# Division moved behind the values' product for the last two tiles of layers 2 and 3, and layer 3's first norm moved ahead in layer 2's quantised product

## The chip, the cores and the metric

One Trainium2 chip, and of it one core. The program is one launch; its metric is the device time of that launch in microseconds (us). The core has five engines with an instruction queue each: PE (TensorE, matrix products; the profile shows its weight loads apart, as PEld), DVE (VectorE), ACT (ScalarE), POOL (GpSimd) and SP (SyncE, which starts transfers). Work that has to cross from one engine to another waits on a semaphore.

## What is computed

Eight steps on x, 4 sequences of 256 tokens with 256 features: four layers, each a gated attention over 64 context tokens and a gated feed-forward part. The change lies in layers 2 and 3:

```python
x = x + tanh(g_xattn[2]) * _L2_xattn_ref(_layernorm(x), ctx, ...)
x = x + tanh(g_ffn[2])   * _L2_ffn_ref(_layernorm(x), weight, bias)
x = x + tanh(g_xattn[3]) * _L3_xattn_ref(_layernorm(x), ctx, ...)     # as layer 2
x = x + tanh(g_ffn[3])   * _L3_ffn_ref(_layernorm(x), ...)            # 8 experts, 2 chosen, 1 shared

def _L2_xattn_ref(q, latent_kv, Wq, Wkv_expand, Wout):                # 16 heads of 16
    qp = q @ Wq.T;  k, v = jnp.split(latent_kv @ Wkv_expand.T, 2, axis=-1)
    scores = jnp.einsum('bhqd,bhkd->bhqk', qh, kh) * inv_sqrt_d
    scores = jnp.where(causal, scores, jnp.finfo(scores.dtype).min)
    out = jnp.einsum('bhqk,bhkd->bhqd', jax.nn.softmax(scores, axis=-1), vh)
    return out.transpose(0, 2, 1, 3).reshape(b, sq, H) @ Wout.T

def _L2_ffn_ref(x, weight, bias):       # int8 rows of x times int8 rows of weight
    x_scale = jnp.maximum(jnp.max(jnp.abs(x), axis=2, keepdims=True) / 127, 1e-12)
    x_q = jnp.clip(jnp.round(x / x_scale), -128, 127)
    return (x_q @ w_q.T) * x_scale * w_scale + bias
```

## The kernel before

**Tiles.** The 1024 tokens are 8 tiles `x[0]` to `x[7]` of 128 tokens by 256 features, which stay in on-chip memory. Tiles 0 to 3 are group 0, tiles 4 to 7 group 1. A norm (`layernorm`, L427) works on a group: statistics on DVE (L432, L435), the root, then the scaling on DVE (L455) or, with `scalar=True`, on ACT (L448 the shift on DVE, L452 on ACT). The root is taken on ACT (L441), or with `powered=True` as a power on POOL (L438, L439).

**Attention in layers 2 and 3** (`attention23`). For each tile: `scores` (L1115 on PE; L1130 maximum and L1132 subtraction on DVE; L1141 exponential on ACT), `weights` (L496 sum over the 64 keys and L497 reciprocal, both on DVE; L501 the multiplication by it, 128x1024 values, on POOL), `transposed_pairs` (8 transposes, L516 on PE, and two copies out of PSUM, L517 on ACT), `context` (the product with the values, L1148 on PE in 8 products of 32 columns each, which the profile shows as 16 instructions; copied out by ACT at L1157) and `output` (L1165 on PE), which `gated_add` (L527 on DVE) adds to x. In the last tile the multiplication L501 is shared: heads 0 to 7 on DVE, 8 to 15 on POOL.

**Order.** `in_flight_parts` (L543) writes the order out by hand: in its turn i it starts the scores of tile i, the weights of tile i-1, and the transposes and context of tile i-2. Up to tile 4 the output follows its own context at once; from tile 6 on it comes after the transposes of the tile behind it. Beside it run generators: in layer 2 the keys and values of layer 3, and in the last turns the norm and the rounding of group 0 for the quantised product (`beside2`). The framework's planner then makes one fixed queue for each engine: what comes first in the program goes first, except where the planner's own timing finds it not ready and something later ready. `behind(a, b)` forces a to stand after b. `kept_busy(n, ...)` puts n products on PE whose result nobody reads.

**The quantised product between them** (`ffn2`, L2062). Group 0 was already rounded in attention 2. Its whole numbers are transposed (L2071 on PE, L2072 on ACT), multiplied (L2080 on PE, `unit`), scaled (L2084 on DVE) and added to x (L2085 on POOL). Then 7 filling products. Then group 1: `rounded(1)` takes its norm, its largest values (L2048), the reciprocal (L2050), the rounding (L2053, L2055, DVE) and adds the bias to x (L2059, POOL); its transposes; then the norm of layer 3 for group 0, then `unit(1, ...)` with 2 filling products, and last the transposes of that norm (L467 on PE, L169 and L171 out) and the queries of layer 3 for group 0 (L482 on PE, L1074 on ACT). Layer 3's first scores need those queries.

**Buffers.** Normed tiles, `y` and `ctxTok` share 7 buffers (tag `xn`), `attn` and `attnT` share 6 (tag `t4`), products in PSUM use 4 single buffers (`mm`) and 2 double ones (`wide`).

## Time and profile before

| what | value |
|---|---|
| median of 3 executions | 822.75 us (818.82, 822.75, 823.13) |
| the profiled execution | 820.13 us, of which the span is 818.3 us |
| PE busy | 773.3 us, 94% of the span |
| DVE, ACT, POOL busy | 502.3, 291.1, 242.9 us |
| granted TensorE clock, mean | 0.996 of full |
| layer 2's scores begin on PE | near 538 us |
| layer 2's last addition to x (L527) | 583.62 us |
| layer 3's first scores (L1115) | 602.70 us |
| layer 3's last addition to x | 646.11 us |
| PE busy, 660 to 680 us | 20.00 of 20 us |

Times inside the span are counted from its start. A row of a timeline gives the start, the length, the engine, the line, the operation, what it writes and reads, how many instructions are merged into the row, and in brackets how long the engine had stood idle and what ended that. A row of waits gives who waited for whom, the sum, the number of waits and the longest. A row of groups gives the busy time and the mean of one instruction in ns.

### The profile page before, as it was taken

The numbers are of one execution on the slowest core, as the hardware profiler recorded it, in microseconds if no ns is written. First come the engines' busy times: TensorE is split into PE (matmuls) and PEld (weight loads), VectorE is DVE, ScalarE is ACT, GpSimd is POOL, SyncE is SP. The second block draws the span as 40 slices with busy tenths as digits, with TensorE's granted clock in tenths as the row PEclk, the third lists the DMA queues.
The fourth block names the chain that finished last, engine by engine and source line by source line (L and its number), as shares of the span: only waits on it lengthen the run. The fifth ranks groups of instructions, "written<-read, shape, count | busy, mean of one in ns | idle before, by whom it ended". The sixth has DMA issues, their size and how long they took to land. (4 is left out here: it accounts for less than half of the span.)

```text
span 818.3 us, 12520 instructions
## 1 busy us (share of the span) xinstructions
PE 773.3 (94%) x4509; PEld 519.4 (63%) x4512; DVE 502.3 (61%) x1154; ACT 291.1 (36%) x506; POOL 242.9 (30%) x214
## 2 busy tenths in 40 slices
PE   6999999899999899999999989999898899999994
PEld 5544433787565677676656565855445647999993
DVE  5565455876694455543878859889879664344331
ACT  2221111443421333332543459166555421233320
POOL 1454544231113244322022110015524103444332
PEclk9999999999999999999999999999999999999998
DMA  9510114800021253333740000450000102222211
GB/s 341 202 40 0 40 58 162 280 37 25 27 65 49 62 123 69 76 79 78 278 177 1 8 1 27 162 204 1 27 0 2 52 9 85 53 48 40 29 18 16
DMA packets 32467, 62.44 MB, mean 76 GB/s; under 512 B 5552, under 2 KB 19504, under 8 KB 31696
## 3 DMA queue, kind: packets, MB, share of 16 engines
q1 hardware_dynamic: 25008, 51.91, 18.5%
q0 software_dynamic: 7104, 9.41, 6.9%
q8 instruction: 39, 0.64, 0.3%
q10 hardware_dynamic: 288, 0.26, 0.1%
q14 instruction: 28, 0.23, 0.1%
HBM read 52.81 MB, written 9.27 MB: 76 GB/s over the span
## 5 line engine op out<-in xcount | busy, mean ns | idle before, releaser
L501 POOL TENSOR_TENSOR attn<-attn,sm 128x1024 f32<-128x1024 f32 (+1 forms) x32 | 55.9, 1750 | 220.4 <-DVE sm L497 176.2
L482 PE MATMUL wide<-xT,big 128*128 128x512 f32 (+1 forms) x240 | 108.6, 600 | 1.1 <-DVE shared L1724 0.9
L782 DVE TENSOR_TENSOR rope<-wide,big 128x512 f32<-128x512 f32 x96 | 59.6, 684 | 52.0 <-PE wide L482 52.0
L482 PEld LDWEIGHTS wide<-xT,big 128*128 128x128 f32 (+1 forms) x240 | 43.4, 188 | 57.3 <-issue 49.3
L1497 PE MATMUL wide<-blk,still 128*128 128x128 f32 x640 | 74.8, 275 | 0.6 <-DVE blk L1469 0.6
L1497 PEld LDWEIGHTS wide<-blk,still 128*128 128x128 f32 x640 | 73.1, 192 | 0.8 <-issue 0.8
L754 PE MATMUL mm<-vo,attnT 128*128 128x256 f32 x256 | 58.6, 382 | 1.6 <-ACT attnT L517 1.2
L482 PE MATMUL wide<-xT,dense 128*128 128x512 f32 (+1 forms) x120 | 55.2, 599 | 0.1
L754 PEld LDWEIGHTS mm<-vo,attnT 128*128 128x128 f32 x256 | 47.8, 190 | 11.5 <-issue 3.0
L517 ACT COPY attnT<-mm 128x512 f32<-128x512 f32 x64 | 34.5, 587 | 37.5 <-PE mm L516 37.1
L496 DVE TENSOR_REDUCE sm<-attn 128x16 f32<-128x1024 f32 x32 | 38.6, 1208 | 12.9 <-ACT attn L490 11.6
L1459 DVE COPY still<-big 128x1024 f32 x20 | 13.9, 693 | 52.0 <-PE wide L1497 44.5
L1531 POOL DMA_INDIRECT out_dram<-ring,scratch x20 | 31.5, 1577 | 39.5 <-DVE ring L1524 15.8
L1531 POOL DMA_INDIRECT sums<-ring,big x17 | 26.8, 1578 | 48.3 <-ACT ring L1613 18.9
L516 PE MATMUL mm<-ident,attn 128*128 128x128 f32 x256 | 34.5, 276 | 5.7 <-POOL attn L501 2.8
L1515 PE MATMUL mm<-big,hidden 128*128 x160 | 37.8, 380 | 1.4 <-DVE hidden L1508 1.4
L1432 POOL DMA_INDIRECT xs<-xd,scratch x20 | 20.0, 1000 | 62.2 <-PE mm L1466 34.1
L516 PEld LDWEIGHTS mm<-ident,attn 128*128 128x128 f32 x256 | 28.7, 141 | 14.6 <-issue 6.1
L1507 ACT ACTIVATE hidden<-wide 128x512 f32<-128x512 f32 x20 | 12.0, 598 | 71.2 <-PE wide L1497 65.7
L482 PEld LDWEIGHTS wide<-xT,dense 128*128 128x128 f32 (+1 forms) x120 | 21.5, 185 | 24.7 <-issue 22.3
L527 DVE SCALAR_TENSOR_TENSOR x<-mm,tg,x 128x256 f32<-128x256 f32 x44 | 20.6, 473 | 21.4 <-PE mm L754 12.7
L836 ACT COPY big<-mm 128x512 f32<-128x512 f32 x16 | 8.6, 589 | 68.0 <-PE mm L824 61.7
(367 smaller groups left out, 1581.8 us busy)
## 6 DMA issues: line engine op xcount, KB each, us to landing
big<-in_L_w_gate_up SPq DMA_DIRECT2D x8, 1024.0 KB, 10.4
big<-in_L_w_down SPq DMA_DIRECT2D x8, 512.0 KB, 10.7
w_L_qk<-in_L_qk SPq DMA_DIRECT2D x4, 896.0 KB, 9.6
big<-in_L_w SPq DMA_DIRECT2D x2, 1480.0 KB, 8.1
big<-in_L_w SPq DMA_DIRECT2D x2, 1110.0 KB, 5.4
big<-in_L_wo SPq DMA_DIRECT2D x1, 2048.0 KB, 15.0
big<-in_L_w SPq DMA_DIRECT2D x2, 1024.0 KB, 5.1
xd<-xn SPq DMA_DIRECT2D x16, 128.0 KB, 1.8
```

Of the source, the lines that this page charges most:

```text
L482: nc.tensor.matmul(ps, w(c), xT[:, c, :], start=(c == 0), stop=(c == 1))
L496: nc.vector.tensor_reduce(sm, e, AX.X, ALU.add)
L501: engine.tensor_tensor(one, one, sm[:, part].unsqueeze(2).to_broadcast(list(one.shape)), ALU.mult)
L516: nc.tensor.transpose(ps[:, i * P : (i + 1) * P], ev[:, pr * P : (pr + 1) * P], ident)
L517: nc.scalar.copy(aT[:, half * 4 : half * 4 + 4, :].rearrange("p i t -> p (i t)"), ps)
L527: return nc.vector.scalar_tensor_tensor(x[t], ps, gate, x[t], ALU.mult, ALU.add)
L754: nc.tensor.matmul(ps[:, :D], aT[:, s, :], vo[:, s, :], start=(s == 0), stop=(s == NP - 1))
L782: nc.vector.tensor_tensor(m[:, s, :].rearrange("q (b t) -> q b t", t=S), ps[:, s, :].rearrange("q (b t) -> q b t", t=S), table, ALU.mult,)
L1432: nc.gpsimd.indirect_dma_start(out=xs, out_offset=None, in_=self.xd, in_offset=bass.IndirectOffsetOnAxis(ap=self.gather[:, b : b + 1].bitc ...
L1497: made = nc.tensor.matmul(ps[:, k, f : f + P], w[:, at : at + P], st[:, c * P : (c + 1) * P], start=(c == 0), stop=(c == 1),)
L1515: made = nc.tensor.matmul(ps[:, :D], hT[:, j * P : (j + 1) * P], self.w[:, bass.ds(r + j * D, D)], start=(j == 0), stop=(j == n - 1),)
L1531: nc.gpsimd.indirect_dma_start(out=self.sums[b % len(self.sums)], out_offset=bass.IndirectOffsetOnAxis(ap=self.scatter[:, b : b + 1].bitca ...
```

## The change

It has three parts.

1. For tiles 6 and 7 of layers 2 and 3, `weights` is not called: the exponentials are transposed undivided. In `context`, behind the product with the values, 8 more products with a constant matrix of zeros and ones (`pair_ones`, 32 columns) put each head's sum, 16 times over, into the other half of the same PSUM buffer; DVE takes the reciprocal of that 128x256 block and multiplies. These take the place of ACT's copy (L1157).
2. The order in `in_flight_parts`: both last tiles are transposed one after the other, and from tile 3 on the output of a tile comes behind the transposes of the next and ahead of its context. In layer 2 one filling product is put ahead of tile 6's context.
3. In `ffn2`, the rounding is split from the scales, and layer 3's norm for group 0 stands ahead of group 1's rounding, and its transposes ahead of `unit(1, ...)`. The 2 filling products behind that unit are left out. The shift of group 1's norm is put behind group 0's second `y`.

```diff
+    pair_ones = const.tile([P, 32], F32, tag="pair_ones", name="pair_ones")
+    nc.gpsimd.memset(pair_ones, 0.0)
+    nc.gpsimd.memset(pair_ones[:64, :16], 1.0)
+    nc.gpsimd.memset(pair_ones[64:, 16:], 1.0)
...
-            nc.vector.scalar_tensor_tensor(shift, mv[:, :, 0], -1.0, rstd, ALU.mult, ALU.mult)
+            made = nc.vector.scalar_tensor_tensor(shift, mv[:, :, 0], -1.0, rstd, ALU.mult, ALU.mult)
+            if late is not None:
+                behind(made, late)
...
-            if 1 <= i <= NT:
-                sums = weights(made[i - 1], shared=i == NT)
+            if 1 <= i <= NT - 2:
+                weights(made[i - 1])
             t = i - 2
-            if 0 <= t < NT:
+            if 0 <= t < NT - 1:
                 aT = turn(made.pop(t))
-            if t >= NT - 2:
+            if t == NT - 2:
+                last = turn(made.pop(NT - 1))
+            if t == NT - 1:
+                aT = last
+            if t >= TPG:
                 add(t - 1)
-                made_x = gated_add(t - 1, outs.pop(t - 1)[:, :D], gate)
-                if t == NT - 2:
-                    behind(made_x, sums)
+                gated_add(t - 1, outs.pop(t - 1)[:, :D], gate)
             if 0 <= t < NT:
                 ctx[t] = context(t, aT)
-            if 0 <= t < NT - 3:
+            if 0 <= t < TPG - 1:
                 add(t)
...
         def context(t, aT):
+            if layer == 2 and t == NT - 2:
+                kept_busy(1, ps_wide()[:, 0], kept["out"])
...
+            if t >= NT - 2:
+                for pr in range(NP):
+                    half, r = divmod(pr, 4)
+                    nc.tensor.matmul(
+                        ps[r * 32 : (r + 1) * 32, 2 * P + half * P : 2 * P + (half + 1) * P],
+                        pair_ones, aT[:, pr, :], start=True, stop=True, tile_position=(0, r * 32),
+                    )
+                nc.vector.reciprocal(cT, ps[:, 2 * P :])
+                nc.vector.tensor_tensor(cT, ps[:, : 2 * P], cT, ALU.mult)
+                return cT
...
-            kept_busy((7, 2)[g], ps_wide()[:, 0], last)
+            if g == 0:
+                kept_busy(7, ps_wide()[:, 0], last)
...
-        xq, xs = rounded(1)
-        xqT = turned(xq)
-        xn = layernorm(0, True)
+        xn, xi, xs = rounded(1, after_y=True)
+        xn_3 = layernorm(0, True)
+        xqT = turned(integers(xn, xi))
+        xT_3 = transposed(xn_3)
         unit(1, xqT, xs)
-        kept[3, 0] = head_queries(3, transposed(xn))
+        kept[3, 0] = head_queries(3, xT_3)
```

`integers` is the loop of L2053 and L2055, taken out of `rounded`; the additions of the bias (L2059) now stand ahead of it in the program.

More of the change, by code (lines that the diff above doesn't have):

```diff
@@ L424, in keep_rows, with layernorm @@
             nc.sync.dma_start(out=tiled(sums, layer)[:, t, :], in_=x[t])
-    def layernorm(g, scalar=False, after=(), powered=False):
+    def layernorm(g, scalar=False, after=(), powered=False, late=None):
         mv = small([P, TPG, 2], "mv")
@@ L516, in transposed_pairs @@
                 nc.tensor.transpose(ps[:, i * P : (i + 1) * P], ev[:, pr * P : (pr + 1) * P], ident)
-            nc.scalar.copy(aT[:, half * 4 : half * 4 + 4, :].rearrange("p i t -> p (i t)"), ps)
+            kept["turned"] = nc.scalar.copy(aT[:, half * 4 : half * 4 + 4, :].rearrange("p i t -> p (i t)"), ps)
         return aT
@@ L1156, in context @@
             cT = sb.tile([P, 2 * P], F32, tag="xn", name="ctxTok", bufs=AHEAD + 2)
+            if t >= NT - 2:
[3 more added lines that the diff above has]
+                        ps[r * 32 : (r + 1) * 32, 2 * P + half * P : 2 * P + (half + 1) * P],
+                        pair_ones,
+                        aT[:, pr, :],
+                        start=True,
+                        stop=True,
+                        tile_position=(0, r * 32),
+                    )
+                nc.vector.reciprocal(cT, ps[:, 2 * P :])
+                nc.vector.tensor_tensor(cT, ps[:, : 2 * P], cT, ALU.mult)
+                return cT
             made = nc.scalar.copy(cT, ps[:, : 2 * P])
@@ L1164, in output @@
             for half in range(2):
-                nc.tensor.matmul(
+                kept["out"] = nc.tensor.matmul(
                     ps[:, :D], cT[:, half * P : (half + 1) * P], w_o[:, half, :], start=(half == 0), stop=(half == 1)
@@ L1178, in beside2 @@
             if i == NT + 1:
-                kept["rounded"] = rounded(0, xn)
+                xn, xi, xs = rounded(0, xn)
+                kept["rounded"] = integers(xn, xi), xs
             next(keys, None)
@@ L2039, in weights2, with rounded @@
         return wqT, scale, bias
-    def rounded(g, xn=None):
+    def rounded(g, xn=None, after_y=False):
         bias = kept["weights2"][2]
-        xn = xn or layernorm(g, True, powered=True)
+        xn = xn or layernorm(g, True, powered=True, late=kept["y"] if after_y else None)
         xs = small([P, TPG], "xs")
@@ L2050, in rounded, with integers @@
         nc.vector.reciprocal(xi, xs)
+        for i in range(TPG):
+            t = g * TPG + i
+            nc.gpsimd.tensor_tensor(x[t], x[t], bias, ALU.add)
+        return xn, xi, xs
+    def integers(xn, xi):
         whole_numbers = []
@@ L2056, in rounded @@
             whole_numbers.append(q)
-        for i in range(TPG):
-            t = g * TPG + i
-            nc.gpsimd.tensor_tensor(x[t], x[t], bias, ALU.add)
-        return whole_numbers, xs
+        return whole_numbers
     def ffn2(gate):
@@ L2083, in unit @@
                 y = sb.tile([P, D], F32, tag="xn", name="y", bufs=AHEAD + 2)
-                nc.vector.scalar_tensor_tensor(y, ps[:, :D], xs[:, i : i + 1], scale, ALU.mult, ALU.mult)
+                made = nc.vector.scalar_tensor_tensor(y, ps[:, :D], xs[:, i : i + 1], scale, ALU.mult, ALU.mult)
+                if i == 1:
+                    kept["y"] = made
                 nc.gpsimd.tensor_tensor(x[t], x[t], y, ALU.add)
-            kept_busy((7, 2)[g], ps_wide()[:, 0], last)
+            if g == 0:
+                kept_busy(7, ps_wide()[:, 0], last)
         xq, xs = kept.pop("rounded")
         unit(0, turned(xq), xs)
-        xq, xs = rounded(1)
-        xqT = turned(xq)
-        xn = layernorm(0, True)
+        xn, xi, xs = rounded(1, after_y=True)
+        xn_3 = layernorm(0, True)
+        xqT = turned(integers(xn, xi))
+        xT_3 = transposed(xn_3)
         unit(1, xqT, xs)
-        kept[3, 0] = head_queries(3, transposed(xn))
+        kept[3, 0] = head_queries(3, xT_3)
     steps = [
```

## The prediction

> **What bounds the kernel now.** I read the page first: PE is busy for 773.3 of 818.3 us, with a granted clock of 0.996. So the time is PE's own work, plus the 45 us in which it stands, and a change gains by closing those gaps or dropping filling products. The table by stretches shows where the gaps in layers 2 and 3 are. Its columns are the stretch, its length, then busy time and instructions of PE, PEld, DVE, ACT and POOL, and at the end the granted clock, the DMA share and GB/s.

> ```profile
> 576.00:580.00 4.00, 2.74 (x30) 1.72 (x29) 3.96 (x13) 3.16 (x8) 2.95 (x5) 1.00 0.00 0
> 592.00:596.00 4.00, 2.27 (x17) 1.45 (x18) 2.48 (x10) 1.94 (x4) 0.46 (x1) 1.00 0.01 2
> ```
> ```profile
> 634.00:638.00 4.00, 3.09 (x39) 2.08 (x36) 3.40 (x7) 2.49 (x5) 1.17 (x2) 1.00 0.00 0
> 642.00:646.00 4.00, 3.32 (x31) 2.28 (x29) 2.39 (x8) 2.02 (x6) 0.00 (x0) 1.00 0.00 0
> ```

> The gaps are the end of layer 2's attention, the rounding of group 1 in the quantised product, and the end of layer 3's attention. At 576 to 580 DVE is full (3.96 of 4) while PE has a third free. From 646 on PE is nearly full to the end (20.00 of 20 at 660 to 680), so what is saved before 646 should reach the end of the kernel.

> The waits from 540 to 660 say who makes PE stand (total us, times, longest):

> ```profile
> PEld mm L1148 <- ACT attnT L517: 10.5, 23, 1.7
> PEld mm L1165 <- ACT ctxTok L1157: 6.9, 10, 0.8
> DVE mx L1130 <- PE wide L1115: 6.5, 5, 2.6
> PEld mm L516 <- POOL attn L501: 4.1, 4, 1.5
> ```

> Rows one and two are a ping-pong: PE transposes, ACT copies, PE multiplies, ACT copies, PE multiplies again. The division on POOL (row four) is the smaller wait. Row three's longest, 2.6 us, is the start of layer 3, where DVE has nothing until the first scores.

> The timeline shows the chain between the layers, first the end of layer 2 and the quantised product:

> ```profile
> 578.50 0.42 PE L1148 MATMUL mm<-attnT,values 128*32 128x128 f32 x8 [1.26 <-ACT attnT L517]
> ...
> 583.62 0.48 DVE L527 SCALAR_TENSOR_TENSOR x<-mm,tg,x 128x256 f32<-128x256 f32 x1 [0.95 <-PE mm L1165]
> ...
> 586.13 0.16 DVE L448 SCALAR_TENSOR_TENSOR shift<-mv,rstd 128x4 f32<-128x4 f32 x1 [1.14 <-POOL rstd L439]
> 586.21 1.65 DVE L2084 SCALAR_TENSOR_TENSOR y<-mm,xs,kept 128x256 f32<-128x256 f32 x4
> ...
> 595.02 2.08 ACT L452 ACTIVATE xn<-x,shift,rstd 128x256 f32<-128x256 f32 x4
> ```

> and, from the window behind it, the first scores of layer 3:

> ```profile
> 602.70 0.73 PEld L1115 LDWEIGHTS wide<-kbd,xT 64*128 64x128 f32 x8 [0.27 <-ACT xT L1074]
> ```

> From the last addition to x in layer 2 to those scores it is 602.70 - 583.62 = 19.1 us. Layer 3's norm is scaled only at 595.02, behind the whole rounding, though its group was complete near 589.6 (the last of L2085).

> **Part 1: the sums.** `pair_ones` costs three fills on POOL at the start, by the fills there 0.1 to 0.2 us each, beside x's load (DVE waits 2.52 us for it): nothing.

> Removed in each layer: on DVE two sums (L496, 1.20) and two reciprocals (0.246), 2.9 us, and its half of tile 7's division (0.77 and 1.54); on POOL 1.9 and 1.05 to 1.5; on ACT two copies of 0.37. Added: on PE 2 x 16 instructions; a context's 16 take 0.64 us, the next starting 0.38 later, so 0.38 each. On DVE two products of a 128x256 PSUM block (0.41, by L1974) and two reciprocals of 128x256, which the trace does not have. Its reciprocals are small (count, then busy us and mean ns):

> ```profile
> L497 DVE RECIPROCAL sm<-sm 128x16 f32<-128x16 f32 x32 | 7.9, 247 | 0.4
> L444 DVE RECIPROCAL rstd<-rstd 128x4 f32<-128x4 f32 x14 | 2.5, 175 | 7.2 <-ACT rstd L441 7.2
> L497 DVE RECIPROCAL sm<-sm 128x8 f32<-128x8 f32 x2 | 0.4, 203 | 0.1
> ```

> From 4 to 16 elements it grows by (247 - 175) / 12 = 6.0 ns an element, six times an ordinary operation (L1130's 1024 elements in 1208 ns). That gives 0.247 + 240 x 6.0 ns = 1.69 us. The low end is an ordinary 128x256 operation, 0.41; the high end the slope from 4 to 8, 7.0 ns, 1.93. I take 1.69, since the three rows lie on one line.

> [...]

> **Part 2: the ends of the attentions.** With the output of a tile between the transposes and the context of the next, PE's two waits per tile have work in them. Packed without waits, from tile 3's context at 566.51 in layer 2: contexts 3 x 0.64, transposes 4 x 1.06, outputs 3 x 1.06, the key product 0.70, the filling product 2 x 0.43, tile 6's context with its sums 1.02, in all 11.9 us, to 578.4. Tile 7's exponentials (571.97 to 573.03 now, sooner without tile 6's sum ahead of them on DVE) are there in time. Then DVE is the chain: 2 x (1.69 + 0.41) = 4.2, to 582.6; with 0.3 for the semaphore the last output starts at 582.9 against 582.45 now. **Layer 2 ends 0.5 us later**; with the reciprocal at 0.41, 1.8 sooner; at 1.93, 1.0 later. What was saved on POOL and ACT comes back as two reciprocals in a row on DVE; behind those queue the outputs, and everything PE has in its queue behind them.

> Layer 3, from 629.77: the same without key and filling product, 10.4 us, plus 0.5 because tile 5 is still divided on POOL until 634.2: 640.7. Plus 4.2 and 0.3: the last output at 645.2 against 644.94. **0.3 later**, bounds 2.1 sooner and 0.8 later.

> **Part 3: between the layers.** Group 1's norm starts 0.5 later with layer 2's end. Its shift now stands behind two of the `y`, which fit into DVE's wait of 1.14 for POOL's power (2 x 0.41), and are gone from behind it. From that shift to the reciprocal of the scales it is 4.5 us now (586.13 to 590.60), with four `y`, four maxima and layer 3's statistics between; 0.8 less, and 0.5 later at the start, makes 590.3. Layer 3's root, reciprocal and shift follow at once instead of behind the rounding: the scaling on ACT runs near 591.2 to 593.2, in ACT's wait of 2.83 us ahead of L2072. The rounding (3.0 us now, slowed to 0.53 and 0.51 an operation while POOL adds the bias) ends at 593.6 as now. The transposes of layer 3 (1.04) lie beside ACT's copies L2072 (1.07), so `unit(1)` starts at 594.8 (594.70 now). Behind its 1.21 us the queries start at 596.0 instead of 598.74; from there to the scores it is 3.96 us now, so 600.0, or with the copies of xT (0.59 and 0.69) not quite done, 600.3. **Layer 3 starts 2.4 us sooner**, layer 2's loss included. Bounds: 0, if the fourth normed tile keeps the old place; 4.0, if the wait ahead of the rounding's transposes closes too. No step moved here issues a DMA, so SP's queue sees nothing; on POOL the bias addition keeps its place behind the four L2085, and the power might stand one 0.73 us addition later.

> The two filling products dropped (4 x 0.43) lie in that same stretch and are in the 2.4. The clock: at 592 to 596, with PE 2.27 of 4 busy, the grant is 1.00, and it is 0.62 only in the last 8.3 us, where PE does nothing. The waits I expect are 1.5 us at most, so the clock costs nothing.

> Group 1's half of layer 3 (its `y`, L2085, statistics) keeps its time; its queries, 606.36 now, are not needed before tile 4. DVE, busy from 603.88 nearly without a break, starts 2.4 sooner and carries that through the layer.

> **Sum.** -2.4 at layer 3's start, +0.3 at its end: -2.1 us, so 818.0 for the profiled execution of 820.13 (its span of 818.3 and 1.8 around it). The three executions have a median of 822.75; the mean of these four is 821.2, and I forecast from that: **819.0**, about 0.3% sooner.

> **The rivals.**
> - *The reciprocals cost little or are covered.* For it: DVE has 1.6 of 4 us free at 642 to 646, and PE can put the next stage's transposes and shared products into the wait. Against it: at 576 to 580 DVE has nothing free. At 0.41 each, both ends give 2.3 to 2.4 more: -2.1 - 4.7 = -6.8, 814.4.
> - *The divisions on DVE become the bound.* In each layer two reciprocals stand in a row ahead of the last output, so the sum is -2.1 + 4 x (r - 1.69): slower than before from r = 2.2 us. For it: six times an ordinary operation is drawn from 16 elements and stretched to 256. At r = 2.7 it is +1.9, 823; more than 0.5% slower needs r = 3.2.
> - *The norm does not come forward.* Four tiles of group 1 and four of layer 3 want 8 of 7 `xn` buffers, so the fourth waits for the transposes of the first (593.6); if the planner then keeps L452 behind L2072, part 3 gives nothing: +0.5 + 0.3, 822.0.

> **Chances.** Forecast, -4.1 to 0: 0.50. Cheap or covered reciprocals, beyond -4.1: 0.32. DVE the bound: 0.10, of which 0.05 beyond +4.1. Norm not forward: 0.08. A change of 0.5% (4.1 us) is about what can be told from none. So faster 0.32, same 0.63, slower 0.05. The range goes from the first rival's end, 814, to the third's 822.0 with 1.5 for the spread of the executions, 823.5.

> **What would show it.** Right: 128x256 reciprocals of 1.6 to 1.8 us; layer 2's last addition near 584; L452 of layer 3 from 591; first scores near 600.3; PE standing 1 to 1.5 us ahead of each of the last two outputs. Wrong: reciprocals far from 1.69; ctx 6 later than 578.4 because ACT's scaling of group 0 (2.08 us) still stands ahead of its copies; DVE unable to carry 2.4 us through layer 3.

## The result, and the profile after

| | before | after |
|---|---|---|
| median of 4 executions | 821.57 us | 829.98 us (828.25 to 832.39) |
| ratio, with its 95% interval | | 1.0111 [1.0081, 1.0141] |
| the profiled execution | 820.13 us | 832.39 us |
| its span, mean granted clock | 818.3 us, 0.996 | 830.6 us, 0.984 |

The change costs 8.4 us. I had forecast a gain of about 2, with a range up to 823.5, so the time is outside it and on the other side.

To compare kernels I cut each trace at four events. A goes from layer 2's first scores on PE to the start of its last addition to x; B from there to layer 3's first scores; C from there to layer 3's last addition. What lies ahead of A scatters by itself (it ends between 534.9 and 539.9 us, in code that no kernel here changes), so the sum A + B + C is what compares. Each trace is of one execution, and those of one kernel lie up to 8 us apart (e1 below: 820.64 us at a granted clock of 0.994, 828.27 at 0.986), so a sum and a ratio of medians need not agree to the microsecond.

| | A | B | C | sum |
|---|---|---|---|---|
| before | 46.13 | 19.08 | 43.41 | 108.62 |
| after | 51.35 | 17.64 | 48.48 | 117.47 |

The sum is 8.85 us more, close to the 8.41 between the medians. **B became shorter by 1.4; both ends of an attention became longer by over 5.** The table by stretches of the kernel after, with the columns of the prediction (the granted clock is the third number from the end), shows both ends:

```profile
580.00:584.00 4.00, 1.19 (x34) 0.91 (x33) 3.72 (x10) 0.00 (x0) 0.00 (x0) 1.00 0.00 0
584.00:588.00 4.00, 2.85 (x36) 2.02 (x36) 2.19 (x4) 0.00 (x0) 0.00 (x0) 0.63 0.02 4
588.00:592.00 4.00, 2.83 (x12) 2.12 (x12) 1.76 (x4) 0.29 (x1) 0.00 (x0) 0.50 0.00 0
```
```profile
652.00:656.00 4.00, 1.55 (x32) 1.09 (x25) 3.27 (x7) 0.00 (x0) 0.00 (x0) 0.83 0.00 0
656.00:660.00 4.00, 4.00 (x14) 2.99 (x15) 2.60 (x7) 0.65 (x2) 0.00 (x0) 0.59 0.38 131
```

At 580 to 584 PE, which bounds this kernel, works 1.19 of 4 us. Behind that, the granted clock is 0.63 and then 0.50, where it was 1.00 in the same stretches of the kernel before. The timeline of the kernel after tells who stands for whom:

```profile
580.04 0.65 PE L1158 MATMUL mm<-attnT,values 128*32 128x128 f32 x16
...
581.61 1.72 DVE L1178 RECIPROCAL ctxTok<-mm 128x256 f32<-128x256 f32 x1
583.36 0.42 DVE L1179 TENSOR_TENSOR ctxTok<-mm,ctxTok 128x256 f32<-128x256 f32 x1
583.93 1.10 PE L1189 MATMUL mm<-w_L,ctxTok 128*128 128x256 f32 x4 [2.81 <-DVE ctxTok L1179]
584.97 1.04 PE L1158 MATMUL mm<-attnT,values 128*32 128x128 f32 x16
...
586.90 1.76 DVE L1178 RECIPROCAL ctxTok<-mm 128x256 f32<-128x256 f32 x1 [0.67 <-PE mm L1170]
588.70 0.42 DVE L1179 TENSOR_TENSOR ctxTok<-mm,ctxTok 128x256 f32<-128x256 f32 x1
589.17 2.08 PE L1189 MATMUL mm<-w_L,ctxTok 128*128 128x256 f32 x4 [2.32 <-DVE ctxTok L1179]
...
591.29 0.48 DVE L533 SCALAR_TENSOR_TENSOR x<-mm,tg,x 128x256 f32<-128x256 f32 x1 [2.17 <-PE mm L1189]
```

The two reciprocals take 1.72 and 1.76 us, as estimated. But they don't stand in a row. PE's queue has the output of tile 6 (583.93) ahead of the context of tile 7 (584.97). The output waits 2.81 us for tile 6's reciprocal and product; tile 7's context, which needs none of it, waits behind it on PE; and so tile 7's reciprocal can begin only at 586.90, 3.6 us after the first was done. Then PE stands 2.32 us once more. From 585 us on, everything PE does is slow: the context takes 1.04 us instead of the 0.65 of tile 6's, the last output 2.08 instead of 1.13 in the kernel before.

### The profile page after: what moved, and what is told of

Same layout as the page of the kernel before. It is cut to its first block, busy times and chain, and to the rows that moved or that the text cites. A ratio compares the mean times of both kernels' runs of the same rounds, so it can differ in the third digit from the quotient of the medians.

```text
span 830.6 us, 12623 instructions
## 1 busy us (share of the span) xinstructions
PE 782.2 (94%) x4574; PEld 526.8 (63%) x4574; DVE 505.4 (61%) x1152; ACT 289.8 (35%) x502; POOL 237.1 (29%) x213
## 5 line engine op out<-in xcount | busy, mean ns | idle before, releaser
L507 POOL TENSOR_TENSOR attn<-attn,sm 128x1024 f32<-128x1024 f32 (+1 forms) x28 | 49.6, 1775 | 211.1 <-DVE sm L503 194.0
L488 PEld LDWEIGHTS wide<-xT,big 128*128 128x128 f32 (+1 forms) x240 | 43.5, 188 | 57.3 <-issue 49.3
L1484 DVE COPY still<-big 128x1024 f32 x20 | 13.9, 694 | 52.0 <-PE wide L1522 44.5
L502 DVE TENSOR_REDUCE sm<-attn 128x16 f32<-128x1024 f32 x28 | 33.9, 1211 | 12.1 <-ACT attn L496 11.6
```

The lines of the kernel that those rows point to most:

```text
L488: nc.tensor.matmul(ps, w(c), xT[:, c, :], start=(c == 0), stop=(c == 1))
L502: nc.vector.tensor_reduce(sm, e, AX.X, ALU.add)
L507: engine.tensor_tensor(one, one, sm[:, part].unsqueeze(2).to_broadcast(list(one.shape)), ALU.mult)
```

## The experiments

**The theory** after this result: (a) the queue puts the two reciprocals one behind the other with a full round by way of PE between them, and (b) PE's standing lowers the granted clock, which stretches its products. Rivals: the reciprocals alone are too dear, in whatever order; the planner's queues have changed elsewhere; or part 3 loses.

| run | A | B | C | sum | ratio to before, 95% interval |
|---|---|---|---|---|---|
| e4, parts 1 and 2 | 51.07 | 20.66 | 48.62 | 120.35 | 1.0110 [1.0080, 1.0139] |
| e3, part 3 alone | 46.15 | 17.33 | 45.66 | 109.14 | 0.9991 [0.9975, 1.0006] |
| e1, context first | 49.09 | 17.31 | 44.30 | 110.70 | 1.0038 [1.0015, 1.0062] |
| e2, filled | 49.76 | 18.80 | 46.59 | 115.15 | 1.0053 [1.0030, 1.0076] |
| e6, copies for reciprocals | 46.93 | 17.30 | 44.03 | 108.26 | not comparable |
| e7, context first and filled | 47.42 | 17.31 | 44.69 | 109.42 | 1.0008 [0.9992, 1.0023] |
| e8, e7 divided in turn | 47.43 | 17.31 | 44.69 | 109.43 | 1.0015 [1.0001, 1.0028] |
| e10, order alone | 44.23 | 21.35 | 42.58 | 108.16 | 0.9996 [0.9979, 1.0013] |
| e5, order and part 3 | 44.22 | 18.59 | 41.98 | 104.79 | 0.9954 [0.9935, 0.9972] |
| e9, e1 with small reciprocals | 44.98 | 17.31 | 41.31 | 103.60 | 0.9916 [0.9889, 0.9943] |
| e11, the same again | 44.98 | 17.30 | 41.30 | 103.58 | 0.9939 [0.9918, 0.9960] |

In e5 and e10 the last two additions of layer 2 follow each other without a gap; the table counts from the second, 0.4 us after the first.

### e4 and e3: which part loses

e4 is the kernel before with parts 1 and 2 of the diff, e3 the kernel before with part 3 alone.

> The kernel before with parts 1 and 2 alone (division behind the product with the values, order of the outputs), the quantised product as before the change. If parts 1 and 2 hold the whole loss and part 3 a gain: layer 2 takes 51.4 us and layer 3 48.5 as in the changed kernel, the stretch between them 19 to 20.5, and the time is 831 to 833, 1.2% to 1.4% over the kernel before. If part 3 is what costs: 822.

> The kernel before with part 3 alone (layer 3's norm ahead of the rounding, its transposes ahead of the second unit, no filling products behind it, the shift behind the second y). My step as predicted: first scores of layer 3 come 2.4 us sooner after layer 2's last addition, 16.7 us instead of 19.1, and the time is about 0.3% less, 819 us. Rival: the fourth normed tile or the queue keeps the old place: 19.1 us and 821.5. In the changed kernel that stretch is 17.6 us with the clock at half in part of it.

Parts 1 and 2 carry the whole loss: e4 has the long ends (51.07 and 48.62) and is as slow as the kernel after. Part 3 takes 1.75 us out of B, but e3 as a whole is no faster: C is 2.25 us longer. The timeline of e3 shows where in layer 3, and the table by stretches shows the clock there:

```profile
629.01 1.06 ACT L1143 ACTIVATE attn<-attn 128x1024 f32<-128x1024 f32 x1 [1.60 <-DVE attn L1134]
629.98 0.35 ACT L1159 COPY ctxTok<-mm 128x256 f32<-128x256 f32 x1
...
630.38 2.07 PE L1167 MATMUL mm<-w_L,ctxTok 128*128 128x256 f32 x4 [2.06 <-ACT ctxTok L1159]
```
```profile
628.00:632.00 4.00, 1.94 (x16) 1.40 (x9) 3.38 (x5) 1.32 (x2) 1.90 (x1) 0.80 0.02 4
```

ACT's queue has the copy of a context behind an exponential that starts only at 629.01. It waits for DVE, whose queue has another order here: between the layer's third addition to x (626.14) and the subtraction for that exponential (627.64) it takes a sum (L498, 626.51); in the kernel before, the subtraction follows the addition directly (630.30 and 630.69). PE waits 2.06 us for the copy and the next output takes 2.07 instead of 1.13. So a start that was 1.75 us sooner was given back in a queue further on. That this order alone made the wait was not tried by a run of its own.

### e1: the context of tile 7 ahead of the output of tile 6

```diff
-            if t >= TPG:
+            if t >= TPG and t != NT - 1:
                 add(t - 1)
                 gated_add(t - 1, outs.pop(t - 1)[:, :D], gate)
             if 0 <= t < NT:
                 ctx[t] = context(t, aT)
+            if t == NT - 1:
+                add(t - 1)
+                gated_add(t - 1, outs.pop(t - 1)[:, :D], gate)
```

> The changed kernel, but in the last turn but one the context of tile 7 and its sums stand ahead of the output of tile 6 (layers 2 and 3). Theory 'queue': the two divisions ran one behind the other with an output and a context between them, since PE had tile 7's context behind an output that waited for DVE. Then tile 7's division follows tile 6's directly: layer 2 from its first scores to its last addition goes from 51.4 us to about 47.4 (46.1 before the change), layer 3 from 48.5 to about 44.2 (43.4 before), the clock stays nearer to full, and the time is about 821 us. Rival 'reciprocal': the two reciprocals of 1.7 us on DVE are the loss whatever the order; then layer ends stay within 1 us of 51.4 and 48.5 and the time is 828 or more.

This is the order that my sum had assumed. A falls by 2.26 us and C by 4.18, so 6.77 of the 8.85 us by which the sum had grown are gone; of the 8.4 us between the medians, 3.4 are left. A was expected at 47.4 and came out 1.7 longer. The timeline of e1:

```profile
577.39 0.62 PE L1161 MATMUL mm<-attnT,values 128*32 128x128 f32 x16
...
578.06 3.34 DVE L1181 RECIPROCAL ctxTok<-mm 128x256 f32<-128x256 f32 x2
581.32 0.69 DVE L1182 TENSOR_TENSOR ctxTok<-mm,ctxTok 128x256 f32<-128x256 f32 x2
581.82 3.65 PE L1192 MATMUL mm<-w_L,ctxTok 128*128 128x256 f32 x8 [3.38 <-DVE ctxTok L1182]
```
```profile
580.00:584.00 4.00, 2.18 (x5) 1.80 (x6) 2.15 (x4) 0.00 (x0) 0.00 (x0) 0.74 0.00 0
```

Both reciprocals now run in a row. But PE waits 3.38 us in one piece, the clock is 0.74 in the stretch behind, and the eight instructions of the two outputs take 3.65 us.

### e2 and e7: keeping PE busy through the wait

e2 is the kernel after with three filling products ahead of each of the four reciprocals; e7 is e1 with four ahead of tile 7's:

```diff
+                    kept["ones"] = nc.tensor.matmul(
...
+                if t == NT - 1:
+                    kept_busy(4, ps_wide()[:, 0], kept["ones"])
                 nc.vector.reciprocal(cT, ps[:, 2 * P :])
```

> The changed kernel with three filling products (6 instructions of 0.43 us, 2.6 us in all) behind the sums of each of the last two tiles, so that PE works through the waits for DVE; the order is left as it is. It tells the fallen clock from the wait itself. Theory 'wait and clock': the clock stays at 1.00, the second context with its sums takes 1.0 us again instead of 1.9 and the last output 1.1 instead of 2.0, but DVE's chain is as long as it was: layer 2 takes about 49.6 us and layer 3 about 46.6, the time is about 825. If the clock were the whole loss: 46 and 43.5, and 820 or less. If the clock were none of it: no change, 830.

> The kernel with tile 7's context ahead of tile 6's output, plus four filling products (8 instructions, 3.4 us) behind the sums of tile 7, where PE stood 3.4 us in layer 2 and 3.0 in layer 3. Theory 'clock': in layer 2 the clock had fallen to 0.74 there and the two outputs took 3.65 us instead of 2.1; now it stays at 1.00 and layer 2 takes 47.4 us instead of 49.1. In layer 3 the clock had held, so 44.3 stays or grows by up to 0.3. Time about 822, 2 us less than without the filling. If the clock were not the cause of the 3.65, layer 2 stays at 49.

The filling products do no work that anyone reads, so only the clock can make them pay. They do: against the kernel after, e2's A is 1.59 us shorter and C 1.89; against e1, e7's A is 1.67 shorter. The same stretch and the outputs in e7:

```profile
580.00:584.00 4.00, 4.00 (x14) 2.33 (x13) 3.02 (x5) 0.00 (x0) 0.00 (x0) 1.00 0.00 0
```
```profile
582.50 1.89 PE L1194 MATMUL mm<-w_L,ctxTok 128*128 128x256 f32 x8
```

The clock is 1.00 and the same eight instructions take 1.89 us. In e7's C the filling brings nothing (44.69 against 44.30): in e1's layer 3 a wait of 3.00 us had left the clock at 1.00. In e2 the low clock came up at another place, in the quantised product, where PE stood only 0.60 us of the 4 from 596 on:

```profile
596.00:600.00 4.00, 3.40 (x19) 1.59 (x18) 1.38 (x6) 3.50 (x7) 0.00 (x0) 0.95 0.00 0
600.00:604.00 4.00, 4.00 (x10) 1.98 (x9) 3.37 (x12) 0.00 (x0) 2.77 (x4) 0.63 0.00 2
```

There the queries of layer 3 take 4.68 us instead of 3.70, and B is 1.2 longer than after's. Why the grant fell there stays open.

### e6: the price of the reciprocal alone

```diff
-                nc.vector.reciprocal(cT, ps[:, 2 * P :])
+                nc.vector.tensor_copy(cT, ps[:, 2 * P :])
```

> The changed kernel, order and all, with a plain copy of the 128x256 PSUM block in place of the reciprocal, so the last two tiles of layers 2 and 3 are multiplied by their sums and not divided by them. It prices the reciprocal in the changed order. A copy takes 0.4 us, a reciprocal 1.73. Theory 'queue and clock': each layer has two reciprocals in one chain, 2 x 1.3 = 2.6 us, and the waits shrink from 2.8 to 1.5 us, so the clock stays up and another 1.5 to 2 us go: layer 2 47.3 us instead of 51.4, layer 3 44.5 instead of 48.5, time about 822. If only the reciprocals themselves count: 48.8, 45.9, and 825. If the reciprocals are beside other work: no change.

Its time as a whole (844.33 us) tells nothing: multiplying by the sums changes the values that choose the experts, and behind C PE has 1167 instructions instead of the 1041 of the kernel after. A, B and C do compare. A copy takes 0.39 us in place of 1.74. The timeline of e6, DVE's copies and PE's two waits for them:

```profile
577.96 0.39 DVE L1178 COPY ctxTok<-mm 128x256 f32<-128x256 f32 x1
...
578.96 1.10 PE L1189 MATMUL mm<-w_L,ctxTok 128*128 128x256 f32 x4 [1.48 <-DVE ctxTok L1179]
...
582.08 1.13 PE L1189 MATMUL mm<-w_L,ctxTok 128*128 128x256 f32 x4 [1.01 <-DVE ctxTok L1179]
```

Waits of 1.48 and 1.01 us leave the clock at 1.00. With e6 the loss in A adds up: the change with a cheap operation in the reciprocal's place costs 0.80 (46.93 - 46.13); two reciprocals in a chain 2 x (1.74 - 0.39) = 2.70; the lower clock 1.75 (tile 7's context and sums, which overlap, 1.88 us together instead of 1.08; the last output 0.95 longer). That makes 5.25; measured is 5.22. In C it is 0.62 + 2.70 + 1.83 (output 0.81, context and sums 0.77, output 0.25) = 5.15; measured is 5.07.

### e8: DVE's own order

```diff
-                nc.vector.reciprocal(cT, ps[:, 2 * P :])
-                nc.vector.tensor_tensor(cT, ps[:, : 2 * P], cT, ALU.mult)
+                made = nc.vector.reciprocal(cT, ps[:, 2 * P :])
+                if t == NT - 1:
+                    behind(made, kept["divided"])
+                kept["divided"] = nc.vector.tensor_tensor(cT, ps[:, : 2 * P], cT, ALU.mult)
```

> e7 with tile 7's reciprocal put behind tile 6's multiplication on DVE (in e1 and e7 DVE takes both reciprocals first, so that tile 6's output waits for both). Theory: tile 6's output goes 1.7 us sooner, and the last output starts right behind DVE's last multiplication instead of behind tile 6's output: layer 2 from 47.4 to 46.5 us, layer 3 from 44.7 to 43.8, a ratio of about 0.9985. Rival: the last output is held by DVE's last multiplication alone, and nothing changes: 47.4 and 44.7, 1.0008.

Tile 6's product is now at 581.05, between the two reciprocals, yet A and C are as in e7: the rival held, though not for the reason that it gave. The four filling products keep PE until 583.1, and both outputs start there. What the order in turn is worth without filling wasn't tried.

### e5 and e10: the order of the outputs, with the old division

Both keep the division on POOL; e10 is the kernel before with this edit alone, e5 has part 3 as well.

```diff
-            if t >= NT - 2:
+            if t >= TPG:
                 add(t - 1)
                 made_x = gated_add(t - 1, outs.pop(t - 1)[:, :D], gate)
...
-            if 0 <= t < NT - 3:
+            if 0 <= t < TPG - 1:
                 add(t)
```

> The kernel before with part 3 and the new order of outputs (from tile 3 on behind the transposes of the next), but with the division as before, on POOL and for tile 7 shared with DVE. It tells whether the order and the earlier norm are worth anything without the new division. If the order closes the two waits per tile as I reckoned: layer 2 about 45.3 us (46.1), layer 3 about 43.5 (45.7 with part 3 alone), time 819. If the waits only move to the next copy or to POOL: 46 and 45.5, time 821.

> The kernel before with the order of part 2 alone (from tile 4 on the output of a tile stands behind the transposes of the next and ahead of its context; division and quantised product as before). Theory: the order itself is the gain, since it fills PE's waits for ACT's copies. Layer 2's first scores to its last addition 43.8 us (46.13 in the kernel before, 43.82 in e5), layer 2's end to layer 3's first scores 19.1, layer 3's first scores to its last addition 42.0 (43.41; e5 41.98): about 3.7 us in all, a ratio near 0.9955. Rival: the order pays only with layer 3's norm ahead, as in e5: then layer 3 stays at 43.4 and the ratio is 0.997 or more.

The order shortens A by 1.9 us in both. Alone it comes to nothing. The ratio is the one that e10's rival gave, but not for its reason: C is 0.83 us shorter, and B 2.27 longer. The waits of e10 from 586 to 602 (who waited for whom, us in total, times, longest) and its table by stretches show why:

```profile
PE mm L2071 <- DVE xn L2055: 2.8, 2, 2.3
```
```profile
588.00:592.00 4.00, 1.22 (x9) 0.46 (x8) 3.67 (x15) 2.14 (x5) 1.92 (x3) 0.98 0.01 2
592.00:596.00 4.00, 3.38 (x12) 1.99 (x12) 2.09 (x5) 3.03 (x6) 1.67 (x3) 0.59 0.01 2
```

PE runs through its seven filling products, then stands 2.3 us before the rounding of group 1 is ready, and the clock is 0.59 in the stretch behind it. Measured from the last addition to x, the transposes of that rounding start 1.16 us later than in the kernel before (10.20 us against 9.04): in e10 DVE takes the four `y` (581.85) ahead of the norm's L438 (583.42), in the kernel before behind it. e5 has a wait of 2.33 us at the same place and the clock at 0.86 and 0.71, but layer 3's norm is transposed beside it, and B comes out 18.59. So here two parts neither of which showed a gain alone (0.9996 and 0.9991, both intervals with 1 inside) came out 0.5% faster together.

### e9 and e11: dividing late with small reciprocals

The wanted gain was to take the division off POOL. e9 is e1 with the sums taken on DVE again (128x16, then the small reciprocal), spread on POOL to 128x256, and brought to PSUM by four PE instructions, so that ACT copies and DVE multiplies:

```diff
+                nc.vector.tensor_reduce(sm, e, AX.X, ALU.add)
+                nc.vector.reciprocal(sm, sm)
+                nc.gpsimd.tensor_copy(spread, sm.unsqueeze(2).to_broadcast([P, NH, D // NH]))
...
+                    nc.tensor.matmul(
+                        pr_[:, half * P : (half + 1) * P], spread[:, half * P : (half + 1) * P], ident, start=True, stop=True
+                    )
-                nc.vector.reciprocal(cT, ps[:, 2 * P :])
+                nc.scalar.copy(cT, pr_[:, : 2 * P])
                 nc.vector.tensor_tensor(cT, ps[:, : 2 * P], cT, ALU.mult)
```

> A third way: the last two tiles' sums and reciprocals are taken while the tokens lie on the partitions (128x16, 1.2 and 0.25 us on DVE, beside PE's transposes), POOL repeats them 16 times, two products with the identity turn them to the features' side, ACT copies them out, and DVE multiplies behind the product with the values; tile 7's context stands ahead of tile 6's output. If the long reciprocals and PE's wait for them are what cost: the last additions come about 3 us sooner than with tile 7's context first alone, layer 2 about 45.5 us, layer 3 about 42.5, clock 1.00, and the time is about 818, under both kernels. If it is the transposing of undivided tiles itself or the order that costs: 49 and 44 as there, and 824.

> e9 once more, beside the order alone on the same chip: if the small reciprocals (128x16, spread over the features by PE) and part 3 are worth something beyond the order, its ratio stays near 0.9916 and below that of the order alone by 0.003 to 0.004.

The timeline of e9:

```profile
576.51 1.13 PE L1196 MATMUL mm<-w_L,ctxTok 128*128 128x256 f32 x4
...
578.73 1.13 PE L1196 MATMUL mm<-w_L,ctxTok 128*128 128x256 f32 x4 [1.08 <-DVE ctxTok L1186]
```

One wait of 1.08 us is left in front of the last two outputs of layer 2 and none in layer 3. The clock is 1.00 at 572 to 608 in e9, and at 620 to 648, the end of layer 3, in e11. Both runs beat the kernel before and the kernel after. Against the order alone (e10) e11 is 0.0057 lower, more than was expected. Against e5, the order with part 3, it is not settled: the sum A + B + C is 1.2 us less, but the intervals of the ratios overlap.

## Why the prediction was wrong, point by point

**The reciprocal of 128x256, 1.69 us: right.** Four were measured, 1.72 to 1.76 us. Two readings beside it were loose: 6.0 ns is five times L1130's 1.18 ns an element, not six, and the three rows bend a little (7.0 ns an element from 4 to 8, 5.5 from 8 to 16).

**"Then DVE is the chain: 2 x (1.69 + 0.41) = 4.2": this step failed.** It takes tile 7's context to run beside tile 6's division, directly behind tile 6's sums. The diff has the output of tile 6 between them, as I had written at the head of the same paragraph, and that output waits for DVE. So the chain is not DVE's two steps but DVE, output, context, sums, DVE again, output. I had left out of the chain an instruction that waits for the very operation I was adding. "Layer 2 ends 0.5 us later" became 5.2, "0.3 later" for layer 3 became 5.1. In e1, with the order that the sum assumed, tile 6's sums end near 577.6 (578.6 when both kernels are counted from layer 2's first scores), against the 578.4 reckoned. DVE begins 0.5 us later than that, behind statistics of x, and takes both reciprocals ahead of both products, so the outputs start together: A is 1.3 and C 1.3 longer than before in e7, at full clock, against 0.5 and 0.3. The 0.3 us that the sum gives the semaphore is in no row: from the end of DVE's product to the output it is 0.15 and 0.05 us in the rows of A above. And 2 x (1.69 - 0.41) is 2.6 us, not the 2.3 to 2.4 of the first rival, so its end lies some 0.4 us lower.

**"The waits I expect are 1.5 us at most, so the clock costs nothing": this step failed with the first.** The waits were 2.81, 2.32, 2.44 and 2.45 us, and the clock cost some 1.8 us in A and as much in C. With the waits of e6 (1.48 and 1.01 us, clock 1.00) it would have been right. One row, PE 2.27 busy of 4 us at a clock of 1.00, was too little to say from where on a wait costs clock; what the traces showed of it stands at the end.

**"Layer 3 starts 2.4 us sooner": the mechanism is right, the size too large.** With 0.5 lost in layer 2, B had to shrink by 2.9; it shrank by 1.75 to 1.78 in e1, e3, e6 and e7. The timeline of e7, in which layer 2's last addition is at 584.43:

```profile
587.68 0.62 DVE L452 SCALAR_TENSOR_TENSOR shift<-mv,rstd 128x4 f32<-128x4 f32 x1
...
594.17 2.08 ACT L458 ACTIVATE xn<-x,shift,rstd 128x256 f32<-128x256 f32 x4 [2.14 <-DVE shift L452]
```

I had put group 1's shift behind two of the four `y`. It runs behind all four and takes 0.62 us instead of 0.16, so it ends 3.87 us after the last addition instead of 2.67. And layer 3's reciprocal and shift do not "follow at once": they stand on DVE behind the first two roundings, and the scaling starts 9.7 us after the last addition (11.4 before), where I had reckoned 7.1.

**"Starts 2.4 sooner and carries that through the layer": wrong with part 3 alone, right with the whole change.** In e3 the time came back as a wait of 2.06 us and a lower clock (0.80 at 628 to 632): layer 3's last exponential starts 34.94 us after its first scores, against 32.20 before. In e1, e6 and e7, where DVE has no sums to take for the last two tiles, it is 31.85; with the old division it is 33.08 in e5, so there some of the lead is lost on DVE, though C as a whole is shorter.

**The rival of the slower side** was DVE's division as the bound, slower only from a reciprocal of 2.2 us on. Its price was too low by the same mistake: it never had PE's queue between the two reciprocals. With that round and the lower clock counted, the measured 1.74 us was enough.

## What to carry to other kernels

When an operation is put between two instructions of one engine's queue, walk the queue in the order of the program: here tile 7's context, which makes the next reciprocal's input, stood on PE behind an output that waited 2.81 us. Reckon then what a stall of the bounding engine does to its clock: behind a wait of 3.38 us it was 0.74 (e1), and 1.00 with four filling products in that wait (e7). A step gained early can be lost in the queues behind it (e3 was 1.75 us ahead in B and 2.25 behind in C), so try such parts together as well as alone.

## What the runs showed of the hardware that was not expected

The granted clock fell after waits of PE that were shorter than I had thought could matter, and the length of the wait alone did not decide it. Waits of 1.48 and 1.01 us left it at 1.00 (e6), and so did one of 3.00 us (e1, layer 3); one of 2.34 us did not (e10).

```profile
588.47:591.88 3.41, 0.85 (x8) 0.46 (x8) 3.20 (x14) 1.65 (x3) 1.45 (x3) 1.00 0.01 2
591.89:595.29 3.40, 2.78 (x12) 1.66 (x11) 1.53 (x5) 3.04 (x6) 0.96 (x2) 0.50 0.01 2
```
```profile
639.91:643.32 3.41, 2.21 (x66) 1.69 (x64) 2.98 (x5) 0.60 (x2) 0.00 (x0) 1.00 0.02 5
643.33:646.73 3.40, 1.61 (x8) 1.47 (x9) 3.40 (x8) 0.00 (x0) 0.00 (x0) 1.00 0.07 24
```

In e10 the wait falls almost wholly into one step, PE works 0.85 us of it, and the next is at 0.50. In e1's layer 3 the longer wait lies across two, with 2.21 and 1.61 us of work, and the clock holds; in its layer 2 the wait of 3.38 us fills one step (0.06 us of work), and it does not (0.74 at 580 to 584). Three traces do not fit. In e2 PE worked 3.40 of the 4 us from 596 on, nearly all ahead of the fall. In e3 and e7 18 products of 128x512 (from 654.39 and 654.46) take 9.63 and 9.67 us, where 18 such take 7.97 in e9, and from 647 on PE has no wait above 0.35 us ahead of them. The cause of these three stays open. My estimate from the other rows is that it depended on where a wait of 2 to 3 us lay among the steps whether it cost clock, and then a part of what e1 (executions at clocks of 0.986 to 0.994) and the kernel after lost to the clock is chance. No run was made to test this.

A reciprocal of 128x256 values from PSUM took 1.72 to 1.76 us on DVE in the kernel after, some 4.5 times a copy of the same block in e6 (0.39 us).
